# E and the slots' softmax transposed by the DMA crossbar as planes of 16-bit halves, with the softmax left undivided

## The chip, the cores and the metric

The kernel runs on one core of a Trainium2 chip. The metric is the device time of one execution in microseconds. All arithmetic is 32-bit floating point.

## The reference

The reference is one layer of gated slot attention followed by a feed-forward layer with a Hadamard transform in its middle, each with a residual and a layer norm behind it. The input x is 2 x 2048 x 512, with 16 heads of 64 key and 128 value channels and 64 slots a head.

```python
z = cumlogsumexp(s, axis=time);  g = exp(z[t-1] - z[t]);  p = exp(s - z)
hk[t] = hk[t-1] * g[t] + k[t] p[t]^T          # 64 keys x 64 slots
ok[t] = q[t] hk[t]
pv[t] = softmax(ok[t])                        # over the 64 slots
hv[t] = hv[t-1] * g[t] + p[t] v[t]^T          # 64 slots x 128 values
ov[t] = pv[t] hv[t]
o = ov * rsqrt(mean(ov**2) + 1e-5) * g_norm_weight * silu(gate)
x = layernorm(x + o @ Wo)
x = layernorm(x + fwht(silu(x W1^T) * (x W3^T)) @ W2^T)
```

## The kernel before

The attention part works on heads in four groups of four (`NG`, `HG`), and inside a group on 16 chunks of 128 positions (`NCB`), both batch entries of a chunk at once. That makes 64 steps. A step's four heads and two batch entries lie in tiles of 128 partitions x 4 x 128 words: `e` holds the exponentials of the slot logits (called E here), `r` the softmax over the slots, both with positions on the partitions. The products with the weights are Strassen-like: seven products a pair of matrices, named `q(1)` to `q(7)`, `v(1)` to `v(7)` and `o(1)` to `o(7)`. Their sums pass through three PSUM tags, c1 with two buffers, c2 and c3 with one; ACT copies the products 1, 5 and 6 out as `kept` (L458) and the product 4 (L460), and DVE adds the others (L463). c1 is used by q(1), q(6), q(7) and q(4) in turn, so q(7) waits for the `kept` copy of q(6).

`run(new, now, before, old)` (L998) writes out by hand the order of one pass of the loop: `now` is the current chunk, `before` the one before it, whose slots' softmax is ready, `old` the one two before, whose output is being finished. PE, DVE, ACT and POOL take their instructions in exactly this order; the order of SP, which issues all transfers, is set by the framework's own scheduling, and SP too is in order. After the four groups the feed-forward part runs, from about 2400 us on.

What the change touches, in the order of a pass:

- q products of `now` (L503). Between q(6) and q(7) stands `r_transposed` of `before` (L647): four PE transposes into a PSUM bank and an ACT copy to `rT`.
- `exp_s` (L508): DVE clamps, ACT exponentiates into `e2` and `e`, POOL adds the carried row `zc` to `e2` (L516).
- v(1), the transposed k, then small 64 x 64 matmuls: `scores` (L580), `scores2` of `before` (L655, reads `eT` and `rT`), `share_of_keys` (L590), `share_of_values` (L667).
- `e_transposed` (L553): four PE transposes into the same bank pair `ps[1]` that the masked scores were read from (L661), and an ACT copy to `eT`. It is used by the next pass.
- `running_sum` (L559), whose last row goes back to `zc` by two small transfers (L568); `slots` (L608), `values` (L678), `state_slots` (L617), `state_values` (L687, reads `rT`).
- `gated` (L696): squares of the values on ACT (L704), products with the gate on DVE (L706), the mean square plus epsilon to the power -1/2 on POOL (L710, L711), the scaling on POOL (L713).
- v(6), v(5), v(2), v(7); `softmax` (L622) on DVE with the exponential on ACT (L634); v(3); `softmax_sum` (L636) on DVE and POOL: the sum (L638), its reciprocal (L639), and the product of r with 1/z on POOL (L640).
- `o_transposed` of `before` (L724): eight PE transposes (L730), copied by ACT to `ob` (L427, L428), with sums on DVE (L432, L433) and POOL (L434, L435). Then `softmax_end` (L642), the product of r with the reciprocal (L644).
- v(4), `tanh` (L537) on ACT, then o(1), o(5) of `before` (L746, with the additions L742 on DVE), `silu` (L541) on DVE, o(2). o(1) reads `ob`. o(3), o(6), o(7), o(4) follow in the next pass. q(2) takes the c3 buffer that o(2) leaves.

Transfers on SP in a pass are the load of x for a later chunk (L473), loads and stores of the output rows (L721, L762), the two of `zc`, and those of the preparation of the feed-forward weights.

Of the kernel before, what the change touches and what calls it, by code (L numbers as in the profile page):

```python
# [8 lines left out]

F32 = mybir.dt.float32  # L10
AF = mybir.ActivationFunctionType
ALU = mybir.AluOpType
AX = mybir.AxisListType
PSUM = bass.MemoryType.PSUM

P = 128
# [4 lines left out]
DV = 128  # L21
M = 64
HG = 4
NG = H // HG
NQ = 4
TH = P // 2
HALVES = (slice(0, TH), slice(TH, P))
# [6 lines left out]
EPS = 1e-5  # L34
# [4 lines left out]
def gated_slot_attention_ffn_kernel(  # L39
# [13 lines left out]
    nc = tc.nc  # L53
# [7 lines left out]
    small = ctx.enter_context(tc.tile_pool(name="small", bufs=4))  # L61
    ident = const.tile([P, P], F32, name="ident")
    make_identity(nc, ident)


    causal3 = const.tile([P, P + TH], F32, name="causal")
    causal = causal3[:, 0:P]
    make_upper_triangular(nc, causal, val=1.0, diag=True)
    nc.gpsimd.tensor_copy(causal3[:, P:], causal3[:, 0:TH])
    mhalf = const.tile([P, 2 * NQ], F32, name="mhalf")  # L70
    nc.gpsimd.memset(mhalf, -0.5)
    gn = const.tile([P, 1], F32, name="gn")
    nc.sync.dma_start(out=gn, in_=gnw.rearrange("(p o) -> p o", o=1))

    half_gn = const.tile([P, 1], F32, name="half_gn")
    nc.gpsimd.tensor_scalar(half_gn, gn, 0.5, 0.0, ALU.mult, ALU.add)

    within = const.tile([P, TH], F32, name="within")
    for h in HALVES:
# [68 lines left out]
    xb, acc, res, h, wt = {}, {}, {}, {}, []  # L148
# [33 lines left out]
    def silu(h, at, src):  # L182
# [9 lines left out]
        gate, lin = v[:, :, :, 0:TQ], v[:, :, :, TQ:]  # L192
        nc.scalar.activation(o, gate, AF.Silu)

# [157 lines left out]
    with ExitStack() as att:  # L352
        keep = att.enter_context(tc.tile_pool(name="keep", bufs=1))
        c2 = att.enter_context(tc.tile_pool(name="c2", bufs=2))
        c1 = att.enter_context(tc.tile_pool(name="c1", bufs=1))
# [5 lines left out]
        ps = [pps.tile([P, 2, 512], F32, name=f"ps{i}") for i in range(2)]  # L361

        def bank(at, width=P):
            return ps[at // 2][:, at % 2].rearrange("p (i t) -> p i t", t=width)
# [8 lines left out]
        within_scores = [ps[1].rearrange("p j (k i t) -> p k j i t", k=2, t=TH)[:, k] for k in range(2)]  # L373
        pn = ps[1].rearrange("p j (k i m) -> p k j i m", k=2, m=M)[:, 1]

        pe = ps[1].rearrange("p j (k i t) -> p k j i t", k=2, t=P)[:, 0]

        hk = [keep.tile([P, NQ, M], F32, name=f"hk{s}") for s in range(3)]  # L380
# [6 lines left out]

        QUARTERS = [(i, j, HALVES[j], s, HALVES[s], HALVES[s ^ j]) for i in range(NQ) for j in range(2) for s in range(2)]
        OPENS = (1, 2, 5)

        def settle(sums):

            nc.scalar.copy(small.tile([P, 1], F32, name="seen", bufs=1), sums)
# [25 lines left out]
        def load_vg(g):  # L419
            return Weights("wvg", wvg[g])  # L420
# [44 lines left out]
        class Step:  # L465
# [42 lines left out]
            def exp_s(self):  # L508
# [3 lines left out]
                if not self.first:  # L512

                    self.e2 = c1.tile([P, NQ, P], F32, name="e2", tag="e2")
                    nc.scalar.activation(self.e2, self.e, AF.Exp)  # L515
                    nc.gpsimd.tensor_tensor(self.e2[0:1], self.e2[0:1], zc, ALU.add)  # L516
                nc.scalar.activation(self.e, self.e, AF.Exp)

# [31 lines left out]
                self.kr = c1.tile([P, NQ, P], F32, name="kr")  # L550
                nc.scalar.copy(self.kr, bank(0))

            def e_transposed(self):  # L553
                for i in range(NQ):
                    nc.tensor.transpose(pe[:, i // 2, i % 2], self.e[:, i, :], ident)
                self.eT = c2.tile([P, NQ, P], F32, name="eT")
                nc.scalar.copy(self.eT.rearrange("p (j i) t -> p j i t", j=2), pe)

            def running_sum(self):  # L559
                p = pch.tile([P, 512], F32, name="running", tag="c1", bufs=2).rearrange("p (i t) -> p i t", t=P)  # L560
# [73 lines left out]
                nc.scalar.activation(r, r, AF.Exp, scale=DK**-0.5)  # L634

            def softmax_sum(self):  # L636
                self.sm = small.tile([P, 2 * NQ], F32, name="sm")
                nc.vector.tensor_reduce(self.sm, self.r8, AX.X, ALU.add)  # L638
                nc.vector.reciprocal(self.sm, self.sm)  # L639
                nc.gpsimd.tensor_tensor(self.r, self.r, self.iz, ALU.mult)  # L640

            def softmax_end(self):  # L642
                smb = self.sm.rearrange("p (h o) -> p h o", o=1).to_broadcast([P, 2 * NQ, M])
                nc.vector.tensor_tensor(self.r8, self.r8, smb, ALU.mult)  # L644


            def r_transposed(self):  # L647
                for i in range(NQ):
                    nc.tensor.transpose(bank(0)[:, i, :], self.r[:, i, :], ident)
                self.rT = c1.tile([P, NQ, P], F32, name="rT")  # L650
                nc.scalar.copy(self.rT, bank(0))

            def scores2(self):
                for i, j, h, s, t, o in QUARTERS:
# [41 lines left out]
            def gated(self):  # L696

                sq = c1.tile([P, 2, NQ, DV], F32, name="sq", tag="big")
                self.gj = self.t2[:, :, HD:].rearrange("p q (j d) -> p j q d", d=DV)

                every = slice(0, P)
                moves = [(0, every, every), (1, HALVES[0], HALVES[1]), (1, HALVES[1], HALVES[0])]
                for j, to, at in moves:
                    nc.scalar.activation(sq[to, j], self.po[j][at], AF.Square)  # L704
                for j, to, at in moves:
                    nc.vector.tensor_tensor(self.gj[to, j], self.po[j][at], self.gj[to, j], ALU.mult)  # L706
                ss = small.tile([P, 2 * NQ], F32, name="ss")
                nc.vector.tensor_reduce(ss, sq.rearrange("p j q d -> p (j q) d"), AX.X, ALU.add)  # L708
                self.state()
                nc.gpsimd.tensor_scalar(ss, ss, 1.0 / DV, EPS, ALU.mult, ALU.add)  # L710
                nc.gpsimd.tensor_tensor(ss, ss, mhalf, ALU.pow)  # L711
                ssb = ss.rearrange("p (j q o) -> p j q o", j=2, o=1).to_broadcast([P, 2, NQ, DV])
                nc.gpsimd.tensor_tensor(self.gj, self.gj, ssb, ALU.mult)  # L713
# [284 lines left out]
        def run(new, now, before, old):  # L998


            def do(step, name, *args):
                if step is not None:
                    getattr(step, name)(*args)

            def main(name, k):

                if now is not None:
                    getattr(now, name)(k)
                elif before is not None:
                    for _ in range(FILL[name, k]):  # L1010
                        next(ups)

            def work_on(place):

                if not changes:
                    y["place"] = place
                    next(pieces[0], None)
# [30 lines left out]
            if changes:  # L1048
                nw["vg"].sums(0, nc.vector)
            main("q", 5)  # L1050
            work_on(3)
            if changes:
                nw["vg"].sums(1, nc.gpsimd)
            main("q", 6)
            do(old, "o", 6)
            do(before, "r_transposed")
            if changes:
                nw["vg"].sums(2, nc.vector)
            main("q", 7)
# [8 lines left out]
            if now is steps[-1]:  # L1068
                wt.append(load_w(0, 0))
                open_x("wqks", OUTER[:3], 3 * P)  # L1070
            do(now, "exp_s")
            do(old, "row_stats", 1)
            for f in late:
                f(0)
# [15 lines left out]
            do(before, "within2")  # L1090
            do(now, "share_of_keys")
            do(before, "share_of_values")
            do(now, "e_transposed")
            do(now, "running_sum")
            do(old, "row_stats", 0)
            do(old, "normalize")
# [35 lines left out]
                nw["o"].sums(2)  # L1132
                nw["o"].sums(3, nc.gpsimd)
            do(before, "o_transposed")
            do(now, "softmax_end")
            main("v", 4)
            if last:
                nw["vg"] = load_vg(g + 1)
            do(now, "tanh")
            if before is not None and before.first:  # L1140
                w["o"] = nw.pop("o")
# [46 lines left out]
    with tc.manual_schedule(  # L1188
# [11 lines left out]
        for u in range(NU):  # L1200
            if u:
                h = {}
# [89 lines left out]
```

## Time and profile before

| | us |
|---|---|
| median of 3 runs | 3513.03 (3512.81 to 3518.43) |
| span of the profiled execution | 3516.1 |
| attention part, about 0 to 2400: PE busy | 2364.9 |
| DVE, ACT, POOL busy in it | 1632.6, 807.1, 618.6 |
| feed-forward part, 2400 to 3516: PE busy | 1091.8 |

Groups of instructions that the change touches (line, engine, what, count, busy us, mean ns):

| line | engine | what | count | busy us | mean ns |
|---|---|---|---|---|---|
| L555 | PE | transposes of e | 256 | 42.0 | 287 |
| L649 | PE | transposes of r | 256 | 38.4 | 273 |
| L557 | ACT | copy to `eT`, 128x512 | 64 | 37.5 | 587 |
| L651 | ACT | copy to `rT`, 128x512 | 64 | 37.5 | 587 |
| L644 | DVE | r times the reciprocal, 128x512 | 64 | 77.9 | 1217 |
| L639 | DVE | reciprocal, 128x8 | 64 | 13.0 | 203 |
| L638 | DVE | sum, 128x512 to 128x8 | 64 | 43.9 | 686 |
| L539 | ACT | tanh, 128x1024 | 64 | 67.7 | 1058 |
| L393 | ACT | copy of 128x1 | 128 | 20.5 | 160 |

How to read it: matmuls are pipelined, so the mean of one is its latency and not the time that it takes from the stream; four transposes start 0.11 us apart. Busy shares are means over parts that have different limits. Idle time of an engine that nothing waits for costs nothing. A timeline row has the start, the time, the engine (PEld is the loading of weights on PE, SPq the issue of a transfer), the line, the operation, output and inputs, the count merged into the row, and in square brackets the idle time before it and what ended it.

### The profile page before, as it was taken

What the parts mean: (1) busy time and instruction counts of PE and PEld (TensorE: products, weight loads), DVE (VectorE), ACT (ScalarE), POOL (GpSimd) and SP (SyncE); (2) the same over time, 40 slices, a digit from 0 to 9 for tenths busy, and PEclk for the clock granted to TensorE, in tenths of its full rate; (3) what the DMA queues carried; (4) which work ended last, traced back from release to release, by engine and by line L of the source; (5) the groups of instructions that cost most, each with busy time, mean ns of one, the idle gap of its engine ahead of it and who ended that gap; (6) DMA issues with size and microseconds to landing.
All of it is one profiled execution on the core that took longest, in us unless ns stands there. A gap on an engine that the chain in (4) does not pass through costs nothing. (4 is left out here: it accounts for less than half of the span.)

```text
span 3516.1 us, 75258 instructions
## 1 busy us (share of the span) xinstructions
PE 3456.7 (98%) x31840; PEld 2702.8 (77%) x31840; DVE 2354.9 (67%) x3940; ACT 957.0 (27%) x1712; POOL 1144.2 (33%) x1069
## 2 busy tenths in 40 slices
PE   8999999999999999999999999998999999999998
PEld 6777777677777677677777777776888888888887
DVE  5777776665666765656766677777666756756756
ACT  3333333333333333333333333332111111111110
POOL 1222223221221331221332222223634643643544
PEclk9999999999999999999999999999999999999999
DMA  5334334221122232122222243347555544445431
GB/s 184 118 113 138 118 119 152 93 72 62 55 66 70 94 96 65 52 66 70 74 99 68 69 140 129 102 160 270 171 179 205 174 161 176 156 151 184 163 135 68
DMA packets 208833, 425.03 MB, mean 121 GB/s; under 512 B 19696, under 2 KB 120432, under 8 KB 207472
## 3 DMA queue, kind: packets, MB, share of 16 engines
q1 hardware_dynamic: 208496, 420.22, 35.7%
q8 instruction: 250, 4.10, 0.5%
q14 instruction: 87, 0.71, 0.1%
HBM read 297.47 MB, written 125.30 MB: 120 GB/s over the span
## 5 line engine op out<-in xcount | busy, mean ns | idle before, releaser
L529 PE MATMUL c<-wvg,xb 128*128 128x512 f32 x1792 | 812.7, 598 | 4.0 <-DVE wvg L412 2.0
L529 PEld LDWEIGHTS c<-wvg,xb 128*128 128x128 f32 x1792 | 322.1, 190 | 369.6 <-issue 291.9
L503 PE MATMUL c<-xb,wqks 128*128 128x128 f32 x3584 | 553.2, 277 | 15.7 <-DMA wqks<-wqks_blocks 9.6
L503 PEld LDWEIGHTS c<-xb,wqks 128*128 128x128 f32 x3584 | 479.9, 193 | 43.7 <-DVE rows L742 21.5
L218 DVE TENSOR_TENSOR accux<-c,accux 128x512 f32<-128x512 f32 x496 | 341.4, 691 | 180.9 <-PE c L237 163.5
L276 PE MATMUL dc<-w2t,hid 128*128 128x256 f32 x1792 | 455.3, 379 | 2.1 <-DVE res L283 2.1
L237 PE MATMUL c<-wvg,xb 128*128 128x256 f32 x1792 | 432.0, 380 | 6.1 <-DVE accux L218 5.3
L742 DVE TENSOR_TENSOR rows<-c,rows 128x256 f32<-128x256 f32 x448 | 181.7, 418 | 335.9 <-PE c L746 331.4
L237 PEld LDWEIGHTS c<-wvg,xb 128*128 128x128 f32 x1792 | 338.8, 190 | 56.9 <-DVE accux L218 9.1
L276 PEld LDWEIGHTS dc<-w2t,hid 128*128 128x128 f32 x1792 | 340.2, 190 | 49.5 <-DVE res L283 3.3
L503 PE MATMUL c<-wqks,xb 128*128 128x128 f32 x1792 | 347.4, 276 | 0.0
L463 DVE TENSOR_TENSOR t<-c,kept 128x384 f32<-128x384 f32 (+1 forms) x384 | 230.6, 611 | 155.6 <-PE c L503 147.5
L237 PE MATMUL c<-wqks,xb 128*128 128x256 f32 x1344 | 325.1, 380 | 5.2 <-DVE accux L218 2.3
L458 ACT COPY kept<-c 128x384 f32<-128x384 f32 (+1 forms) x384 | 203.5, 530 | 457.8 <-PE c L503 369.5
L516 POOL TENSOR_TENSOR e<-e,zc 1x512 f32<-1x512 f32 x60 | 76.4, 1273 | 710.0 <-ACT e L515 710.0
L237 PEld LDWEIGHTS c<-wqks,xb 128*128 128x128 f32 x1344 | 253.9, 190 | 44.0 <-DVE accux L218 5.0
L503 PEld LDWEIGHTS c<-wqks,xb 128*128 128x128 f32 x1792 | 273.0, 193 | 0.0
L283 DVE TENSOR_TENSOR res<-dc,res 128x256 f32<-128x256 f32 x448 | 189.2, 423 | 117.9 <-PE dc L276 107.3
L573 DVE RECIPROCAL iz<-z 128x256 f32<-128x256 f32 x128 | 223.9, 1749 | 44.6 <-ACT z L564 44.6
L710 POOL TENSOR_SCALAR ss<-ss 128x8 f32<-128x8 f32 x64 | 12.7, 198 | 685.3 <-DVE ss L708 685.3
L706 DVE TENSOR_TENSOR t<-po,t 64x512 f32<-64x512 f32 (+1 forms) x192 | 131.6, 685 | 95.6 <-ACT sq L704 94.3
L252 POOL TENSOR_TENSOR accw<-accw,accux 128x512 f32<-128x512 f32 x64 | 80.8, 1276 | 275.7 <-DVE accux L218 274.3
(189 smaller groups left out, 4975.7 us busy)
## 6 DMA issues: line engine op xcount, KB each, us to landing
xb<-w13s SPq DMA_DIRECT2D x112, 896.0 KB
xb<-xd SPq DMA_DIRECT2D x48, 896.0 KB
yd<-rows SPq DMA_DIRECT2D x128, 256.0 KB
w2t<-w2s SPq DMA_DIRECT2D x32, 896.0 KB
rows<-yd SPq DMA_DIRECT2D x100, 256.0 KB
xd<-xb SPq DMA_DIRECT2D x16, 896.0 KB
wvg<-fxd SPq DMA_DIRECT2D x16, 896.0 KB
w13s<-inner SPq DMA_DIRECT2D x96, 128.0 KB
```

The source lines that it names most:

```text
L218: nc.vector.tensor_tensor(into[:, b], s, (into if first is None else first)[:, b], ALU.add)
L237: nc.tensor.matmul(s[:, j * TQ : (j + 1) * TQ], lhsT=w[:, LEFT[k], j, :], rhs=right[:, RIGHT[k], :], start=(k in (1, 2, 5) and j == 0), st ...
L252: (nc.gpsimd if u or m == 6 else nc.vector).tensor_tensor(o, o, t["u"][:, b], ALU.add)
L276: nc.tensor.matmul(s, lhsT=h["hid"][:, i, LEFT[m], k * P : (k + 1) * P], rhs=h["w2"][:, i, RIGHT[m], :], start=(m in (1, 2, 5) and i == 0) ...
L283: nc.vector.tensor_tensor(r, s, r, ALU.add)
L458: nc.scalar.copy(self.kept[k], s)
L463: nc.vector.tensor_tensor(t[:, to], s, self.kept[other], ALU.add)
L503: nc.tensor.matmul(out[:, i * P : (i + 1) * P], lhsT=a, rhs=b, start=(k in OPENS and c == 0 and i == 0), stop=(c == 1), skip_group_check=True,
L529: nc.tensor.matmul(out, lhsT=self.xb[:, RIGHT[k], c, :], rhs=w["vg"].t[:, LEFT[k], c, :], start=(k in OPENS and c == 0), stop=(c == 1), sk ...
L573: nc.vector.reciprocal(self.iz[:, h], self.z[:, h])
L706: nc.vector.tensor_tensor(self.gj[to, j], self.po[j][at], self.gj[to, j], ALU.mult)
L742: nc.vector.tensor_tensor(y_, self.uo.sum(k), y_, ALU.add)
```

## The change

E and r are no longer transposed on PE. Each 32-bit word is split into its two 16-bit halves, the lower halves of a whole tile in one plane and the upper ones in another (`parts`: on POOL for E, on ACT for r). One DMA transpose a tile, issued from SP, sends both planes through the crossbar, which moves 16-bit elements, and an ACT copy joins the halves again (`e_joined`, `r_joined`). E's split is issued behind `exp_s` and joined in the next pass between q(5) and q(6). r's split is issued after v(4) and joined in the next pass where the PE transposes were.

r is no longer divided by its sum. The values come out larger by the factor of that sum, and so does the root of their mean square: epsilon times the square of the sum is added to the mean square in place of epsilon. That is `floor`: three small squares on ACT in `softmax_sum` (three since the two heads of a pair lie at different halves of the partitions), and one addition on POOL in `gated`. The reciprocal and the product on DVE go. The scratch that the program reserves for software-made DMA descriptors is set to 2048 bytes a partition.

```diff
+U16 = mybir.dt.uint16
...
-        pe = ps[1].rearrange("p j (k i t) -> p k j i t", k=2, t=P)[:, 0]
...
+        MOVES = [(0, slice(0, P), slice(0, P)), (1, HALVES[0], HALVES[1]), (1, HALVES[1], HALVES[0])]
+
+        def words(t):
+            return t.rearrange("p i t -> p (i t)").bitcast(U16).rearrange("p (c h) -> p h c", h=2)
...
-            def e_transposed(self):
-                for i in range(NQ):
-                    nc.tensor.transpose(pe[:, i // 2, i % 2], self.e[:, i, :], ident)
-                self.eT = c2.tile([P, NQ, P], F32, name="eT")
-                nc.scalar.copy(self.eT.rearrange("p (j i) t -> p j i t", j=2), pe)
+            def e_split(self):
+                parts = c1.tile([P, 2, NQ * P], U16, name="parts")
+                nc.gpsimd.tensor_copy(parts, words(self.e))
+                self.et = c1.tile([P, 2 * NQ, P], U16, name="et")
+                nc.sync.dma_start_transpose(out=self.et, in_=parts.rearrange("p h c -> p (h c)"))
+
+            def e_joined(self):
+                self.eT = c1.tile([P, NQ, P], F32, name="eT")
+                nc.scalar.copy(words(self.eT), self.et.rearrange("p (h i) t -> p h (i t)", h=2))
...
             def softmax_sum(self):
-                self.sm = small.tile([P, 2 * NQ], F32, name="sm")
-                nc.vector.tensor_reduce(self.sm, self.r8, AX.X, ALU.add)
-                nc.vector.reciprocal(self.sm, self.sm)
+                sm = small.tile([P, NQ, 2], F32, name="sm")
+                nc.vector.tensor_reduce(sm.rearrange("p q j -> p (q j)"), self.r8, AX.X, ALU.add)
                 nc.gpsimd.tensor_tensor(self.r, self.r, self.iz, ALU.mult)
-            def softmax_end(self):
-                smb = self.sm.rearrange("p (h o) -> p h o", o=1).to_broadcast([P, 2 * NQ, M])
-                nc.vector.tensor_tensor(self.r8, self.r8, smb, ALU.mult)
-            def r_transposed(self):
-                for i in range(NQ):
-                    nc.tensor.transpose(bank(0)[:, i, :], self.r[:, i, :], ident)
+                self.floor = small.tile([P, 2, NQ], F32, name="floor")
+                for j, to, at in MOVES:
+                    nc.scalar.activation(self.floor[to, j], sm[at, :, j], AF.Square, scale=EPS**0.5)
+            def r_split(self):
+                parts = c1.tile([P, 2, NQ * P], U16, name="parts_r")
+                nc.scalar.copy(parts, words(self.r))
+                self.rt = c1.tile([P, 2 * NQ, P], U16, name="rt")
+                nc.sync.dma_start_transpose(out=self.rt, in_=parts.rearrange("p h c -> p (h c)"))
+
+            def r_joined(self):
                 self.rT = c1.tile([P, NQ, P], F32, name="rT")
-                nc.scalar.copy(self.rT, bank(0))
+                nc.scalar.copy(words(self.rT), self.rt.rearrange("p (h i) t -> p h (i t)", h=2))
...
-                nc.gpsimd.tensor_scalar(ss, ss, 1.0 / DV, EPS, ALU.mult, ALU.add)
+                nc.gpsimd.tensor_scalar(ss, ss, 1.0 / DV, 0.0, ALU.mult, ALU.add)
+                nc.gpsimd.tensor_tensor(ss, ss, self.floor.rearrange("p j q -> p (j q)"), ALU.add)
                 nc.gpsimd.tensor_tensor(ss, ss, mhalf, ALU.pow)
...
             main("q", 5)
+            do(before, "e_joined")
...
             do(old, "o", 6)
-            do(before, "r_transposed")
+            do(before, "r_joined")
...
             do(now, "exp_s")
+            do(now, "e_split")
...
             do(before, "share_of_values")
-            do(now, "e_transposed")
             do(now, "running_sum")
...
             do(before, "o_transposed")
-            do(now, "softmax_end")
             main("v", 4)
...
+            do(now, "r_split")
             do(now, "tanh")
...
-    nc = bacc.Bacc("TRN2", target_bir_lowering=False, num_devices=1)
+    nc = bacc.Bacc("TRN2", target_bir_lowering=False, num_devices=1, dynamic_dma_scratch_size=2048)
```

More of the change, by code (lines that the diff above doesn't have):

```diff
@@ L699, in gated @@
                 self.gj = self.t2[:, :, HD:].rearrange("p q (j d) -> p j q d", d=DV)
-                every = slice(0, P)
-                moves = [(0, every, every), (1, HALVES[0], HALVES[1]), (1, HALVES[1], HALVES[0])]
-                for j, to, at in moves:
+                for j, to, at in MOVES:
                     nc.scalar.activation(sq[to, j], self.po[j][at], AF.Square)
-                for j, to, at in moves:
+                for j, to, at in MOVES:
                     nc.vector.tensor_tensor(self.gj[to, j], self.po[j][at], self.gj[to, j], ALU.mult)
```

## The prediction

> **What bounds the kernel now.** I read the page's parts 1 and 2 first, then PE's waits, then one step of the chunk loop in the timeline, and last the group rows for prices.
>
> ```profile
> PE 3456.7 (98%) x31840; PEld 2702.8 (77%) x31840; DVE 2354.9 (67%) x3940; ACT 957.0 (27%) x1712; POOL 1144.2 (33%) x1069
> PEclk9999999999999999999999999999999999999999
> PE c L746 <- ACT ob L427: 5.0, 8, 1.3
> PE c L503 <- DVE rows L742: 5.2, 9, 1.2
> SPq L721 <- DMA yd<-rows: 173.0, 73, 6.0
> ```
>
> PE is busy for 98% of the span at a full granted clock, and the longest waits in its list are a few us each over the whole run. So work taken from PE is worth its full price, and any new wait of PE costs its full length. The loop takes about 37.6 us a step (L730 comes at 1529.07 and again at 1566.68). A step, where the change touches it:
>
> ```profile
> 1504.32 0.48 ACT L458 COPY kept<-c 128x384 f32<-128x384 f32 x1 [0.86 <-PE c L503]
> 1504.98 0.60 PE L649 MATMUL ps<-ident,r 128*128 128x128 f32 x4
> 1505.42 0.61 PE L503 MATMUL c<-xb,wqks 128*128 128x128 f32 x4
> 1513.42 0.56 PEld L580 LDWEIGHTS ps<-t 64*64 64x64 f32 x32 [0.33 <-issue]
> 1515.99 0.42 PEld L555 LDWEIGHTS ps<-ident,e 128*128 128x128 f32 x4 [0.31 <-DVE a L661]
> 1516.48 1.03 PE L562 MATMUL running<-e,causal 128*128 128x256 f32 x4
> 1517.44 0.56 PEld L608 LDWEIGHTS ps<-e,a 64*64 64x64 f32 x32 [0.33 <-ACT eT L557]
> ...
> 1529.07 1.08 PE L730 MATMUL ps<-ident,t 128*128 128x128 f32 x8
> 1529.99 1.88 PE L529 MATMUL c<-wvg,xb 128*128 128x512 f32 x4
> 1530.55 0.63 ACT L634 ACTIVATE r<-r 128x512 f32<-128x512 f32 x1 [5.84 <-DVE r L633]
> 1531.09 0.57 ACT L427 COPY ob<-ps 128x512 f32<-128x512 f32 x1
> 1531.21 0.69 DVE L638 TENSOR_REDUCE sm<-r 128x8 f32<-128x512 f32 x1 [0.16 <-ACT r L634]
> 1531.71 2.85 PE L746 MATMUL c<-wo__11903,ob 128*128 128x256 f32 x12
> 1531.90 0.33 SPq L473 DMA_DIRECT2D xb<-xd  x1
> 1532.04 1.29 POOL L640 TENSOR_TENSOR r<-r,iz 128x512 f32<-128x512 f32 x1 [3.04 <-DVE sm L638]
> ```
>
> The reader should see two things. The transposes L649 and L555 sit in an unbroken PE stream. And just before L746, ACT runs the exponential (L634) and at once the copy of `ob` (L427), which PE consumes 0.05 us after it ends, while DVE is still summing the exponentials: that sum ends at 1531.90, 0.19 us after PE has begun L746. At the other steps the sum ends 0.19 us after L746 begins in the first three groups of heads and 0.14 us after in the fourth.
>
> **What is removed from PE.** Four r transposes: 1504.98 to 1505.42, 0.44 us. Four E transposes: 1515.99 to 1516.48, 0.49 us. Ahead of them PE waits for L661 to free the bank: the last L667 matmul starts 0.34 us before L555, where the same change of tile size elsewhere (L687 to L529) takes 0.20, so 0.14 us goes too. The 0.33 before L608 stays, since L580 has the same 0.33 with no releaser. Removed: 1.07 us a step. On ACT the copies L651 and L557 (587 ns each) go, on DVE the reciprocal L639 (203) and the product L644 (1217): both come after the sum. DVE's relief is worth little: at some 40 steps PE waits 0.14 us in the q stage for L742, which stands behind silu on DVE. With DVE freed I count that 0.14 as gone, 0.09 us a step on average.
>
> **What is added, and what hides it.** (1) The split of E on POOL, 1024 elements: below, a 128x64 copy took 0.23 us; above, L713 took 1.90 for 1024 elements with two inputs. POOL is idle from 1513.33 (end of L516) to 1525.10, so neither end reaches the path. (2) On POOL one 128x8 addition ahead of the power, about 0.2 us by L710's 198 ns, with 0.08 of gap. L713 now ends only 0.07 us before L730, so L730 would slip 0.28; a longer wait comes 2.6 us later and contains it, so I count nothing; without that wait it would cost 0.28 x 62 = 17 us. (3) The r split on ACT, as long as L539's 128x1024 (1.06 us), is put after v's copy L460 and before tanh. Its POOL input (L640) is done before ACT gets there. It pushes tanh to 3.1 us and silu's end to 4.3 us after L746's start; L742 of o(2) ends at 4.75, q(2) needs it at 4.9. Hidden by 0.15 us; what is queued behind it on ACT is q(1)'s `kept` copy, due at 4.1. (4) Joining E on ACT stands between the `kept` copies of q(5) and q(6). The former ends 1503.46; plus 1.06 gives 1504.52, so the q(6) copy ends 1505.02 rather than 1504.80, and q(7) starts 1505.08 instead of 1504.98, its new natural place after the r transposes go: 0.10 us of stall. Bounds: at L458's 0.58 for 512 words, none; at twice L539, 1.2. I take 0.10. (5) Joining r on ACT replaces L651 and is 0.47 longer; nothing of PE's waits for it there, unless its transfer is late (below).
>
> (6) The three squares `floor` on ACT. In the built order they stand after L634 and before L427. They need DVE's sum, so ACT, and the `ob` copies queued behind, now wait for it, and L746 behind these. From L746's present start: sum 0.19, releaser to ACT 0.03 (L634 to L638), three squares, two gaps of 0.02 as between the L704 squares, 0.02, the copy 0.57, and 0.05 to PE. A square of four elements: L517 (512) took 632 ns and L539 (1024) 1058, a line that reaches 0.21 at four elements; below, L393's one-element copy took 0.16; above, L428 (256) took 0.38. With 0.21 the first L746 starts 0.19 + 0.03 + 0.63 + 0.04 + 0.02 + 0.57 + 0.05 = 1.53 us late. DVE's chain to the sum starts at PE's L687 and moves along with it, so earlier PE work doesn't widen this.
>
> The Trainium skill (ScalarE: Activation LUTs, What ACT_TABLE_LOAD costs) says that an immediate-scale ACTIVATE has 186 ns fixed and that back-to-back ones overlap by 93 ns. By that the three squares are an estimated 0.38 us and the stall 1.24; the L704 squares here follow each other with a gap of 0.02 and no overlap.
>
> (7) Two crossbar transposes of 256 KB on SP. E's is issued about 1515 and stands before the later yd store, row load and the two zc transfers (issued 1518.20, needed by L516 some 30 us later); its result is joined 25 us later. r's stands behind L473's xb load and ahead of the row load; it is issued 2.1 us after L746's start. Its join must begin by 14.0 us after it, since then L460 (ending 1510.12, and v(1) starting 1510.31 needs its bank) would be late: 11.9 us of room. The trace has no such transfer. Below: SP's waits for a plain 256 KB yd store (the last line of the first block) are 173.0 us in 73, 2.4 us each. Above: the trace's packets of 4 bytes took 9 ns, and 131,072 of them over 16 engines would be 74 us. The built instruction moves blocks of 16 rows, so pieces of 32 bytes: 8,192 over 16 engines at 9 to 19 ns (4 and 256 byte packets) are 4.6 to 9.6 us. I take 6 us: hidden.
>
> The Trainium skill (VectorE: DVE Perf Modes, The three transpose paths and Rules for kernel authors) speaks against the change: 390 ns on TensorE against 1309 ns through the crossbar for 128x128 of 16 bits, with TensorE preferred where PSUM will do. Eight in a row are an estimated 10.5 us, still inside the room.
>
> **Sum.** -1.07 - 0.09 + 1.53 + 0.10 = +0.47 us a step, x 62 steps that have both a current and a preceding chunk: +29 us. The profiled execution spans 3516.1, so 3545; the runs' median 3513.03 is 3.1 lower, so 3542. The FFN part (from about 2400 us) is untouched. Ends: squares at 0.16 and no q(7) stall, +0.22 a step, 3527; squares at 0.38, +0.98, 3574.
>
> **Rivals.** *The gate is cheap* (faster): the squares overlap or the sum comes earlier. Even squares of no length leave the wait for the sum: 0.19 + 0.03 + 0.02 + 0.57 + 0.05 = 0.86. With no q(7) stall the step is then 1.16 - 0.86 = 0.30 better, 19 us, 3494. It decides from three squares under 0.3 us together. For it: only the extrapolation prices them. Against: the 0.16 of L393 three times is 0.48. *The crossbar is late* (slower): r lands more than 11.9 us after issue, ACT stands in the join, and the copy L460 and v(1) behind it. Each us over is 62 us; at 20 us, 8 x 62 = 500, 4040. For it: the 74 us bound; against: the 16-row blocks. *The change moves nothing*: gate and removed transposes cancel, squares at 0.16 and L730's or q's slack taken up elsewhere, 3513. For it: the terms are equal in kind and each known to about 0.15 us a step, 9 us.
>
> **How the numbers follow.** The gate as costed 0.66, cheap gate 0.12, crossbar late 0.11, cancelling 0.11. A measurement of this kernel can tell about 0.2%, 7 us, from no change. Faster: 0.12, the cheap gate. Same: 0.11 plus 0.03 from the low end of the gate, 0.14. Slower: 0.74. The range reaches from 3510, within the cancelling case, to 3580, above the gate's high end; the likeliest case alone has 3527 to 3574. Outside are the cheap gate and the late crossbar.
>
> **What would show it.** In PE's waits a new row of L746's line behind the `ob` copy, near 62 times and 1.2 to 1.6 us each, some 95 us in all; ACT's idle before `floor` ended by the sum on DVE. The 512 PE transposes of L555 and L649 gone. q(7) behind ACT's `kept` by about 0.1 us. If PE's new waits are instead behind the join of r, the crossbar is late; if L746 waits under 0.9 us, the gate was cheap and the forecast is wrong.

## The result, and the profile after

The changed kernel takes 3563.5 us (median of 4 runs, 3560.8 to 3564.2) against 3514.5 for the kernel before, measured beside it: a ratio of 1.013 (95% interval 1.0116 to 1.0145). The profiled execution spans 3561.4 us, 45.3 more than before.

The page's first part and, from PE's and ACT's lists of waits (total us, times, longest), the rows that are new:

```profile
PE 3430.7 (96%) x31328; PEld 2659.9 (75%) x31328; DVE 2289.2 (64%) x3812; ACT 1126.2 (32%) x1968; POOL 1196.5 (34%) x1197
```
```profile
PE c L758 <- ACT ob L431: 77.0, 63, 4.0
...
PE c L533 <- DVE t L717: 7.5, 12, 0.7
```
```profile
ACT floor L652 <- DVE sm L647: 49.9, 64, 2.0
```

PE has 512 instructions fewer and 26 us less to do, and yet the span is longer: PE stands still. L758 is o(1) (L746 before), L431 the copy to `ob` (L427 before), L647 the sum. The second row, v (L533) behind the gate's products (L717), is all in the fourth group and comes up again in experiment 4. The step that the prediction showed, after the change (timeline):

```profile
1549.05 1.09 PE L742 MATMUL ps<-ident,t 128*128 128x128 f32 x8
...
1549.98 1.88 PE L533 MATMUL c<-wvg,xb 128*128 128x512 f32 x4
...
1550.20 0.63 ACT L643 ACTIVATE r<-r 128x512 f32<-128x512 f32 x1 [5.78 <-DVE r L642]
...
1550.86 0.69 DVE L647 TENSOR_REDUCE sm<-r 128x8 f32<-128x512 f32 x1
1551.58 0.64 ACT L652 ACTIVATE floor<-sm 128x4 f32<-128x4 f32 x3 [0.75 <-DVE sm L647]
...
1552.24 0.58 ACT L431 COPY ob<-ps 128x512 f32<-128x512 f32 x1
...
1552.88 2.86 PE L758 MATMUL c<-wo__12005,ob 128*128 128x256 f32 x12 [1.02 <-ACT ob L431]
```

Read down ACT: the exponential ends at 1550.83, ACT waits 0.75 us for DVE's sum, does three squares, and only then the copy that o(1) needs. Before, the copy began 0.09 us before the exponential's end.

To see where the rest of the 45 us lies, I took the starts of PE's stages out of the timeline of all 62 steps, here the median step of each group of heads and the sum over all steps, after less before:

| stretch on PE | before, groups 1, 2, 3, 4 | after | sum over 62 steps, us |
|---|---|---|---|
| o transposes to o(1) | 2.63, 2.64, 2.64, 2.59 | 3.84, 3.84, 3.84, 4.00 | +78.8 |
| o(1) to the k transposes (the q stage; r was transposed here) | 17.06, 17.68, 17.91, 17.65 | 16.60, 17.45, 17.45, 17.47 | -28.1 |
| scores2 to `slots` (E was transposed here) | 3.51 in all | 2.98 in all | -31.6 |
| `slots` to v(6) | 2.94 in all | 2.94 to 3.15 | +1.6 |
| v(6) to the next o transposes | 8.69, 8.69, 8.69, 9.01 | 8.94, 8.94, 8.94, 9.61 | +19.9 |
| before the first and after the last step | | | +5.4 |

In groups 2 and 3 the q stage has two lengths, since about half of the steps there also prepare feed-forward weights on PE; their medians are of the longer kind. The stretch from the k transposes to scores2 is 1.91 in both kernels.

These make 46.1 (PE's first to last start). A step in the first group grew from 36.75 to 37.22 us, the +0.47 of the forecast; in the fourth group it grew by 1.30.

The prices of the new work (groups of instructions, each shape apart: busy us, mean ns, idle time before them) and SP's issue of the crossbar transfers (ns min/median/max):

```profile
L664 ACT COPY rT<-rt 128x1024 uint16<-128x1024 uint16 x64 | 86.9, 1358 | 0.1
L566 ACT COPY eT<-et 128x1024 uint16<-128x1024 uint16 x64 | 86.5, 1352 | 0.0
...
L658 ACT COPY parts_r<-r 128x1024 uint16<-128x1024 uint16 x64 | 68.3, 1068 | 0.2 <-POOL r L648 0.2
...
L652 ACT ACTIVATE floor<-sm 64x4 f32<-64x4 f32 x128 | 26.1, 204 | 1.5
...
L652 ACT ACTIVATE floor<-sm 128x4 f32<-128x4 f32 x64 | 13.2, 206 | 49.9 <-DVE sm L647 49.9
```
```profile
L562 SPq DMA_TRANSPOSE et<-parts x64: 1232/1242/2719, 24.6 to 2421.5; - x64
```

The joins have no idle time before them that a transfer ended: ACT never waited for the crossbar. By the trace's packets (1024 of 256 bytes a transfer) r's transfers had landed 2.6 us after their issue in the median and 7.7 at worst, E's 3.4 and 5.9.

### The profile page after: what moved, and what is told of

The parts are those of the page before. It is cut to its first block, busy times and chain, and to the rows that moved or that the text cites. A ratio compares the mean times of both kernels' runs of the same rounds, so it can differ in the third digit from the quotient of the medians.

```text
span 3561.4 us, 74715 instructions
## 1 busy us (share of the span) xinstructions
PE 3430.7 (96%) x31328; PEld 2659.9 (75%) x31328; DVE 2289.2 (64%) x3812; ACT 1126.2 (32%) x1968; POOL 1196.5 (34%) x1197
## 5 line engine op out<-in xcount | busy, mean ns | idle before, releaser
L533 PE MATMUL c<-wvg,xb 128*128 128x512 f32 x1792 | 812.9, 598 | 10.9 <-DVE t L717 7.5
L533 PEld LDWEIGHTS c<-wvg,xb 128*128 128x128 f32 x1792 | 322.3, 190 | 376.3 <-issue 292.3
L507 PE MATMUL c<-xb,wqks 128*128 128x128 f32 x3584 | 554.8, 277 | 12.3 <-DMA wqks<-wqks_blocks 8.9
L507 PEld LDWEIGHTS c<-xb,wqks 128*128 128x128 f32 x3584 | 482.5, 192 | 48.2 <-ACT kept L462 23.1
L754 DVE TENSOR_TENSOR rows<-c,rows 128x256 f32<-128x256 f32 x448 | 189.7, 423 | 420.1 <-PE c L758 413.8
L507 PE MATMUL c<-wqks,xb 128*128 128x128 f32 x1792 | 347.2, 275 | 0.0
L507 PEld LDWEIGHTS c<-wqks,xb 128*128 128x128 f32 x1792 | 273.0, 193 | 0.0
L717 DVE TENSOR_TENSOR t<-po,t 64x512 f32<-64x512 f32 (+1 forms) x192 | 131.6, 685 | 95.6 <-ACT sq L715 94.4
```

What stands on the lines that cost most here:

```text
L507: nc.tensor.matmul(out[:, i * P : (i + 1) * P], lhsT=a, rhs=b, start=(k in OPENS and c == 0 and i == 0), stop=(c == 1), skip_group_check=True,
L533: nc.tensor.matmul(out, lhsT=self.xb[:, RIGHT[k], c, :], rhs=w["vg"].t[:, LEFT[k], c, :], start=(k in OPENS and c == 0), stop=(c == 1), sk ...
L754: nc.vector.tensor_tensor(y_, self.uo.sum(k), y_, ALU.add)
```

## The experiments

Times are medians; "before" is the kernel before, run beside each. Experiments 1, 2, 4 and 5 were run together, as were 6 to 9, and 10 and 11.

**1. The gate away.** The squares are moved behind tanh:

```diff
+            def floors(self):
+                sm = self.sm
                 self.floor = small.tile([P, 2, NQ], F32, name="floor")
...
             do(now, "tanh")
+            do(now, "floors")
```

> The changed kernel with the three squares (floor) moved behind tanh on ACT, out of the way of the copies to ob. Theory (the gate in front of o(1) is the loss): the stretch from the o transposes to o(1) falls from 3.84 us back to 2.64 in the first three groups, and PE's waits for ACT's ob copy from 77.0 us to under 10. But ACT then reaches r's split earlier, which stands ahead of tanh and reads POOL's product; that ends some 1.6 us after o(1) starts, so tanh, silu and o(2)'s additions come later and up to 0.65 us a step can go to a wait of q(2). The 0.25 us that POOL's addition costs stays. So 3563 - 1.2 x 62 = 3489 with no new wait and 3529 with all of it. Rival (the crossbar transfers and the joins are the loss, and the gate merely shows up where something else would): 3555 to 3570, with the wait turning up at another line.

Measured: 3488.6 against 3519.0 before, ratio 0.992 (0.9904 to 0.9934), 75 us less than the changed kernel. PE's wait for the copy (L762 is o(1) here):

```profile
PE c L762 <- ACT ob L431: 4.3, 5, 1.2
```

The stretch to o(1) is back at 2.65 us. Of the feared wait of q(2) little came: r's split waits 0.52 us for POOL in the median, and the weight loads of q wait 19.8 us in 42 for o(2)'s additions, a row that the changed kernel doesn't have. That makes the q stage 6.3 us longer over all steps than in the changed kernel, and still 0.3 us a step shorter than before. One thing, the place of three squares, turns the change from a loss into a gain. The 0.26 that the o transposes come late stayed.

**2. The gate alone.** The undivided softmax and its floor, with E and r transposed on PE as before (the diff less `e_split`, `e_joined`, `r_split` and `r_joined`).

> The kernel before with only the undivided softmax and its floor; E and r are still transposed on PE. Theory: nothing is taken from PE, and each step pays the gate (1.20 us in front of o(1), 1.41 in the fourth group) and POOL's addition (0.25 in front of the o transposes): 1.45 to 1.5 x 62 = 90 to 93 us more, 3604 to 3608. Rival (the crossbar part is the loss): not over 3520. Prediction's own sums: 1.53 x 62 = 95 less 0.09 x 62 for the DVE product that goes, 3603.

Measured: 3608.4 against 3519.0, ratio 1.0258 (1.0243 to 1.0273), 89 us more.

```profile
PE c L750 <- ACT ob L433: 81.1, 63, 4.0
```

The loss is there in full without a single crossbar transfer. The stretch to o(1) is 3.89 us in groups 1 to 3 and 4.07 in the fourth, the o transposes come 0.26 late in groups 1 to 3 and not at all in the fourth. The setting of the scratch, which is in every changed kernel, was not tried by itself; it is in this one too, where the gate explains the loss.

**3. What the gate consists of.** The squares stay where the change put them and read the row maxima:

```diff
-                    nc.scalar.activation(self.floor[to, j], sm[at, :, j], AF.Square, scale=EPS**0.5)
+                    nc.scalar.activation(self.floor[to, j], mx[at, :, j], AF.Square, scale=EPS**0.5)
```

> The changed kernel with the three squares where the change put them, but reading the row maxima, which DVE finished before the exponential, in place of the sums: the floor's value is another, the work is the same, and only ACT's wait for the sum is gone. It splits the gate in two. Theory (the gate is a wait of 0.75 us for the sum and 0.64 us of squares, of which PE's own work up to o(1) covers 0.19): the squares then begin 0.02 after the exponential ends, the copy follows, and o(1) starts 1.78 + 0.02 + 0.64 + 0.02 + 0.58 + 0.06 = 3.10 us after the o transposes where it was 3.84: 0.74 x 62 = 46 us less, 3518. Rival (the squares are the price, the wait lies beside other work): 3550 or more. Rival 2 (the wait is all of it): 3490.

Measured: 3501.6 against 3517.0, ratio 0.996 (0.994 to 0.997): 62 us less than the changed kernel, where 46 were expected and 73 by the rival that gives the wait all of it. The stretch to o(1) is 2.97 us, so the wait for the sum was 0.87 of the 1.20, and the squares the remaining 0.33. In the timeline the step has

```profile
1513.61 0.63 ACT L643 ACTIVATE r<-r 128x512 f32<-128x512 f32 x1 [5.78 <-DVE r L642]
1514.14 0.62 ACT L653 ACTIVATE floor<-mx 128x4 f32<-128x4 f32 x3
1514.79 0.59 ACT L431 COPY ob<-ps 128x512 f32<-128x512 f32 x1
```

and shows what was missed: the first square begins 0.10 us before the exponential ends. So the wait for the sum cost this overlap besides its own length: 0.75 and 0.10 of the 0.87. The sum over the steps falls by 54 us (0.87 x 62); 6 of the other 8 lie in the drain after the last step, the rest is not traced to one place.

**4. E alone.** The kernel before with E through the crossbar, the softmax divided and r transposed on PE (`e_split` and `e_joined` of the diff alone).

> The kernel before with only E sent through the crossbar; the softmax is divided and r is transposed on PE. Theory (in the fourth group DVE bounds the stretch from scores2 to v(2), elsewhere PE does): 0.53 us a step in the 47 steps of the first three groups and nothing in the fourth, less 0.1 a step if q(7) waits for the join: 3514 - 20 to 25 = 3489 to 3494. Rival 1 (PE bounds everywhere): 0.53 x 62 = 33 us, 3481. Rival 2 (the transfers disturb other work): 3514 or more.

Measured: 3486.9 against 3519.0, ratio 0.992 (0.990 to 0.993), 32 us less. In the medians that is what the rival gives that lets PE bound everywhere; but its baseline was 5 us above the one that the expectation started from, and the interval of 6 us to either side doesn't tell the two apart. The steps do. The stretch of E falls by 0.53 us in every step; in groups 1 to 3 the step falls by as much (36.75 to 36.21 in the first), and in the fourth it stays at 37.60. There v(6) to the o transposes grew by the same 0.53. Over all steps the two sum to -32.9 and +6.1. DVE in such a step (timeline), with the first and last row of the same chain in the kernel before behind it:

```profile
2120.62 0.69 DVE L594 TENSOR_TENSOR a<-ps,within 128x512 f32<-128x512 f32 x1 [0.70 <-PE ps L665]
2121.23 0.68 DVE L671 TENSOR_TENSOR a<-ps,within 128x512 f32<-128x512 f32 x1
2121.83 0.94 DVE L612 TENSOR_TENSOR hk<-hk,pk 128x256 f32<-128x256 f32 x2
2122.68 0.68 DVE L612 TENSOR_TENSOR hv<-hv,ps 128x512 f32<-128x512 f32 x1
2123.28 0.69 DVE L87 BATCH_NORM_STATS2 st<-rows 128x6 f32<-128x512 f32 x1
2124.01 0.18 DVE L89 BATCH_NORM_AGGREGATE mv<-st 128x2 f32<-128x6 f32 x1
2125.14 1.00 DVE L96 TENSOR_SCALAR rows<-rows,mv,lrs 128x512 f32<-128x512 f32 x2 [0.95 <-POOL lrs L92]
2126.05 1.75 DVE L583 RECIPROCAL iz<-z 128x256 f32<-128x256 f32 x1
2127.72 2.05 DVE L716 TENSOR_TENSOR t<-po,t 128x512 f32<-128x512 f32 x3
```
```profile
2128.40 7.13 PE L534 MATMUL c<-wvg,xb 128*128 128x512 f32 x16 [0.59 <-DVE t L716]
```
```profile
2150.68 0.69 DVE L584 TENSOR_TENSOR a<-ps,within 128x512 f32<-128x512 f32 x1 [0.70 <-PE ps L655]
...
2157.77 2.05 DVE L706 TENSOR_TENSOR t<-po,t 128x512 f32<-128x512 f32 x3
```

From the masked scores (L594) to the gate's products (L716) DVE has no gap but the wait for POOL inside the normalization of the output rows, which is only there in the fourth group. PE then waits for the first of these products. In the kernel before the same chain from the same start takes 7.09 us (L584 to L706), here 7.10: what is taken from PE behind the chain's start can't move its end.

**5. Both through the crossbar, softmax divided.** The kernel before with both transposes through the crossbar; there is no floor, and the division stays. r's split is put behind tanh:

```diff
             do(now, "tanh")
+            do(now, "r_split")
```

> The kernel before with both E and r sent through the crossbar; the softmax is divided as before, so there is no floor, and r's split stands behind tanh on ACT since DVE's product ends some 2.9 us after o(1) starts. Theory: 0.53 x 47 + 0.45 x 62 = 53 us less, 3461; if q(7) waits for the joins 0.1 a step, 3467. If the split holds up the kept copy of q(1), due 4.1 us after o(1) starts, up to 0.3 a step more, 3486. Rival (the transfers are the loss): 3540 or more.

Measured: 3473.7 against 3519.0, ratio 0.988 (0.986 to 0.989), 45 us less: the gain is smaller than either of the first two forecasts. E gives 0.53 a step again, the q stage only 0.28 where r's four transposes had taken 0.44 (experiment 9 finds the rest).

**6. The crossbar twice.** The changed kernel with each transfer issued again into a tile that nothing reads:

```diff
                 nc.sync.dma_start_transpose(out=self.et, in_=parts.rearrange("p h c -> p (h c)"))
+                nc.sync.dma_start_transpose(out=twice, in_=parts.rearrange("p h c -> p (h c)"))
```

> The changed kernel with each of the 128 crossbar transfers issued twice, the second into a tile that nothing reads. Theory (the transfers are hidden: they land 2.6 and 3.4 us after issue, 12 to 25 us ahead of their joins): same time within 0.2%, 3556 to 3570, with no wait of ACT for a transfer. Rival (the transfers or SP's issue of 1.25 us each take part in the loss, by contention or by delaying the other transfers): each us that they cost would cost again, 3590 or more.

Measured: 3565.3, against 3563.5 with one of each. The second issues on SP (min/median/max ns, then first and last start) took 1.87 us for E in the median where the first take 1.23:

```profile
L564 SPq DMA_TRANSPOSE twice<-parts x64: 1261/1868/3807, 25.8 to 2425.8; - x64
```

and no stretch of the step changed by more than 0.01 us in the medians of the groups, `slots` to v(6) aside, which scatters. A second set of transfers costs nothing here that the runs can tell.

**7. One operation less on POOL.** On top of experiment 1, the mean's division by 128 goes into ACT's squares:

```diff
-                    nc.scalar.activation(sq[to, j], self.po[j][at], AF.Square)
+                    nc.scalar.activation(sq[to, j], self.po[j][at], AF.Square, scale=DV**-0.5)
...
-                nc.gpsimd.tensor_scalar(ss, ss, 1.0 / DV, 0.0, ALU.mult, ALU.add)
                 nc.gpsimd.tensor_tensor(ss, ss, self.floor.rearrange("p j q -> p (j q)"), ALU.add)
```

> The kernel with the squares behind tanh, and one operation less on POOL: the squares of the values are scaled by 1/128 on ACT, so that POOL only adds the floor and takes the power, as many operations as before the change. Theory (POOL's added operation stands on the chain to the o transposes in the first three groups, where they come 0.26 us later; in the fourth group DVE bounds this stretch): 0.26 x 47 = 12 us less than the 3488.6 measured with the squares behind tanh, 3476; the o transposes then come 8.69 us after v begins in the first three groups and still 9.4 to 9.6 in the fourth. Rival (the 0.26 has another cause, such as POOL's split of E): 3489, stretch still 8.95.

Measured: 3485.9 against 3488.6 in experiment 1, where 3476 was expected; beside the kernel before the ratios are 0.991 and 0.992, so no gain is clear of noise. The 0.26 went as expected (v(6) to the o transposes 8.69 in groups 1 to 3), but in the first and third group the q stage grew by 0.29. The row of PE's waits that grew from 3.4 us in 7 waits:

```profile
PE c L507 <- DVE rows L757: 11.2, 41, 0.7
```

q(2) now waits for o(2)'s additions, which stand on DVE behind silu, which waits for tanh, which stood behind r's split on ACT. As long as POOL's addition held up the o transposes, this chain had more time: one stall had covered part of another. In experiment 11, with tanh ahead of the split, the row is down to 0.9 us in 3 waits.

**8. The normalization later.** Experiment 5 with the normalization of the output rows (fourth group) moved on DVE behind the gate's products:

```diff
-            do(old, "normalize")
-            do(old, "store_rows")
...
             do(before, "gated")
+            do(old, "normalize")
+            do(old, "store_rows")
```

> The kernel with both through the crossbar and the softmax divided (3473.7), with the normalization of the output rows, which is there in the fourth group alone, moved on DVE from behind the running sum to behind the products with the gate. Theory (in the fourth group DVE bounds the stretch from the second scores to v(2): its wait of 0.95 for POOL and the two normalizations of 1.0 stand ahead of the gate's products): v(2) no longer waits, and the step of that group falls by about 0.53 us, from 37.32 to 36.8, x 13 steps = 7 us: 3467. Rival (what E saves is lost in the fourth group to something else, such as the transfers): step stays 37.3, 3474. Were DVE's sum of the exponentials to become late instead, the o transposes to o(1) would grow over 2.6 us.

Measured: 3484.3, 11 us more than experiment 5 (ratios to before 0.9905 and 0.9877); 7.6 us of the difference lie in the steps and 5.7 after the last one. v no longer waits (9.54 to 8.69 in the fourth group), and o(1) comes 0.89 later after the o transposes (2.59 to 3.48):

```profile
PE c L761 <- ACT ob L432: 12.5, 17, 1.2
```

The softmax's exponential now stands behind the normalization through DVE's order, and the `ob` copies behind the exponential, so the same row as in the changed kernel is back. Both sides were thus partly right: DVE does bound the way to v(2), and the saving does not stay, since DVE bounds the way to o(1) as well. Moving work along an engine that bounds the whole stretch gained nothing.

**9. E's join behind r's.** On top of experiment 5:

```diff
             main("q", 5)
-            do(before, "e_joined")
...
             do(before, "r_joined")
+            do(before, "e_joined")
```

> The kernel with both through the crossbar and the softmax divided (3473.7), with the join of E moved on ACT from between the kept copies of q(5) and q(6) to behind the join of r. Theory (the join of 1.36 us delays the kept copy of q(6), which q(7) waits for, since r's transposes no longer stand between them): the stretch from o(1) to the k transposes falls by 0.11 us a step, from 17.37 to 17.26 in the fourth group, x 62 = 7 us: 3467. Rival (the missing part of r's saving lies elsewhere): 3474, stretch unchanged. The joins then end at most 3 us after the kept copy and are needed some 8 us after it, so no new wait.

Measured: 3462.0 against 3473.7 in experiment 5; the q stage is 0.22 us shorter, twice what was expected. Experiment 5, PE from o(6) into q(7), then the same in experiment 9:

```profile
2099.00 1.03 PE L761 MATMUL c<-wo__17417,ob 128*128 128x256 f32 x4
2099.98 0.71 PE L508 MATMUL c<-xb,wqks 128*128 128x128 f32 x4
2100.53 0.39 PE L508 MATMUL c<-wqks,xb 128*128 128x128 f32 x2
```
```profile
2090.76 1.03 PE L761 MATMUL c<-wo__17417,ob 128*128 128x256 f32 x4
2091.62 0.61 PE L508 MATMUL c<-xb,wqks 128*128 128x128 f32 x4
2092.07 0.39 PE L508 MATMUL c<-wqks,xb 128*128 128x128 f32 x2
```

q(7) starts 0.98 after o(6) with the join in between and 0.86 without; and its first four matmuls then take 0.55 up to the next group in place of 0.45. Here a wait of 0.12 costs 0.22. It stands in the list of the weight loads, again experiment 5 and then 9; the changed kernel has the same row (23.1 us in 64):

```profile
PEld c L508 <- ACT kept L463: 23.1, 64, 0.8
```
```profile
PEld c L508 <- ACT kept L463: 1.5, 2, 0.8
```

**10. The normalization on POOL.** On top of experiment 9, in the fourth group:

```diff
-                        normalize(self.rows[b], self.stats[b])
+                        nc.gpsimd.tensor_scalar(self.rows[b], self.rows[b], *self.stats[b], ALU.subtract, ALU.mult)
```

> The kernel with both through the crossbar, the softmax divided and E's join behind r's (3462.0), with the two normalizations of the output rows (fourth group alone) on POOL instead of DVE. POOL is idle for 6.0 us there; at the 1.28 us of its 128x512 product the two take some 2.6. Theory (DVE bounds the whole way from the second scores to the exponential of the softmax in the fourth group, so that only taking work from it gains there): both its wait for POOL of 0.95 and the two normalizations of 1.0 go; v to the o transposes falls from 9.54 to the 8.69 of the other groups without the o transposes to o(1) growing, step from 37.11 to 36.26, 0.85 x 13 = 11 us: 3451. Rival (as when the normalization was moved on DVE, 0.89 of it comes back in front of o(1)): 3460 or more.

Measured: 3457.4 against 3462.0 in experiment 9; ratio to before 0.983 (0.982 to 0.984). That lies between the 3451 expected and the 3460 at which the rival began, and the medians alone don't decide. The stretches do: the step of the fourth group falls from 37.11 to 36.34 us (36.26 expected), v(6) to the o transposes to 8.69, and o(1) loses only 0.06 of it. So DVE did bound this group. Of the 10 us that this stretch gives over the group, the span has 6 and the median 5: the part after the last step took 3.2 back, and whether that is scatter, the granted clock of the drain or a cost of POOL's slower work (2.08 us each, below) isn't settled.

**11. The same, undivided.** Squares behind tanh and r's split, one operation on POOL, E's join behind r's, the normalization on POOL:

```diff
             do(now, "tanh")
+            do(now, "r_split")
+            do(now, "floors")
```

> The same arrangement with the softmax left undivided: squares and r's split behind tanh, the floor as POOL's only addition, E's join behind r's, normalization on POOL. It tells what leaving out the division is worth once neither gate nor waits stand in its way. Theory: DVE's 1.4 us a step for reciprocal and product lie beside PE and are worth little, at most the 4.8 us in which PE waits for the additions of o behind silu in the divided form: 3446 to 3451, that is 0 to 5 below the divided form. Rival (the division bounds something): over 8 us below it. Rival 2 (the squares still cost): above it.

Measured: 3442.7 us (3438.8 to 3443.2) against 3517.0 before, ratio 0.979 (0.978 to 0.980). It is the fastest of all, 2.1% below the kernel before and 3.4% below the changed one, and 15 us below the divided form, where at most 5 was expected. The sum over the q stage fell by 14.0 us. The waits that went are not in PE's list but in that of its weight loads; the divided form (experiment 10) has

```profile
PEld c L508 <- DVE rows L757: 20.9, 43, 1.3
```

and the undivided form (there L507) 2.7 us in 4. The expectation had looked at the matmuls' row alone (4.7 us in 9). The gain is not the same everywhere: 0.23 us in most steps of the first and third groups, 0.5 to 0.9 in most steps around a change of group, and nothing in half of the second group and nearly all of the fourth, where this wait was not there.

## Why the prediction was right, and where it was not

It said slower, by 29 us, through a wait of o(1) behind the `ob` copy. It is slower by 45 to 49, through that wait.

**The gate** was right in mechanism and nearly in size. Its 1.53 us held the 0.28 by which L730 slips; measured, o(1) comes 1.20 after that and the slip is 0.25 (experiment 2 has both without a crossbar): 1.45 in groups 1 to 3. Summed over all steps that is 78.8 + 48 x 0.25 = 91 us against 95 (48 of the 62 steps; in the 14 of the fourth group another chain bounds the way to the o transposes). The squares took 0.204 us each against 0.21. Of the two prices weighed for them, the L704 row was right: three took 0.64, with no overlap among them, so the 93 ns of the Trainium skill (ScalarE: Activation LUTs, What ACT_TABLE_LOAD costs) is not seen there. It is seen, at 0.10, between the exponential and what follows it without a wait (experiment 3). That the slip is contained in the later wait held too: its price without this cover, given as 17 us, would have been smaller by what experiment 7 found hidden under it.

**E's transposes** were the step that failed. The prediction wrote that PE is busy 98% of the time, "so work taken from PE is worth its full price", and multiplied by 62. The 0.63 was 0.53: of the two changes of tile size it removed, the first running-sum matmuls pay 0.10 for one (1.06 us to `slots`, from 1536.04 to 1537.10, in place of 0.96). And in the fourth group, 14 of the steps, it was worth nothing, because DVE bounds the way from the scores to v(2) there (experiments 4 and 10). 39.1 us were counted; -31.6 + (19.9 - 12.0) = -23.7 came, 12.0 being the slip of 48 x 0.25. The view of before had shown it: this stretch took 9.01 us in the fourth group and 8.69 in the others, so PE was already being held there by 0.32.

**r's transposes, the join and DVE's relief** came out right in sum (-26.7 counted, -28.1 measured) by luck: two errors cancelled. The join before q(6)'s copy costs 0.22, not 0.10 (it takes 1.35 us, not 1.06, and the wait slows the matmuls behind it; experiment 9). DVE's relief is worth 0.23 a step, not 0.09 (14.0 us over 62 steps, experiment 11). The wait is in before's list of the weight loads:

```profile
PEld c L503 <- DVE rows L742: 21.5, 43, 1.6
```

The prediction counted 0.14 at some 40 such steps; taking the wait away gave 0.23 at most of them, and more around the changes of group. Both prices come from other arrangements (experiment 11 also moves the squares and frees r's split from DVE's product), and the changed kernel doesn't part them; but experiment 2, which has the relief and no join, shortens the q stage by 12.0 us over the steps.

That r's split is hidden by 0.15 us held only while the gate stood in front: with the gate gone, q(2) waited for what lies behind the split (experiment 1), and for longer with POOL's operation gone too (experiment 7).

**The crossbar** was hidden, with more room than assumed: landed 2.6 and 3.4 us after issue, 7.7 at worst, where 6 was taken and 11.9 to spare; issuing each twice changed nothing clear of noise. The 6 came from 8,192 pieces of 32 bytes, and the trace shows 1,024 packets of 256. The Trainium skill's figure for one block (VectorE: DVE Perf Modes, The three transpose paths), by which eight in a row would be an estimated 10.5 us, gives over three times what these transfers took. Its advice to transpose on TensorE where PSUM will do (the same page, Rules for kernel authors) doesn't hold here, where PE bounds and SP and the DMA engines don't: both through the crossbar alone gained 45 us (experiment 5).

**The rest of the difference.** Of the 16.3 us by which the span missed (3545 against 3561.4), E is 15.4, the gate -4, r's part -1, and the ends with `slots` to v(6) 7, less 0.8 by which PE's starts grew more than the span. The other 5 between 3542 and the measured median is which executions were compared: the profiled one of before was 3.9 above the median of its four, that of after at its own, and the median of three that the prediction started from was 1.5 below that of four. So of the 20 us between 29 and 49, E makes 15 and the choice of executions about 5; the rest nearly cancels.

## What to carry to other kernels

Read the bound of each stage, not of the whole: a stage that is longer in one part of the loop than in another, with PE doing the same in both, is held by something else, and what is taken from PE there is worth nothing. Before an instruction is put into an engine's order, ask what it waits for and what stands behind it: three 0.2 us squares cost 79 us in front of a copy that PE needs, of which nearly three quarters were the wait, and left no such wait when they stood behind it. Look for waits in the rows of the weight loads too, and when a stall is removed, ask which chain had been living off its time.

## What the runs showed of the hardware

A copy of 128x1024 16-bit elements on ACT takes 1.07 us when it reads with a stride of two and writes densely (L658), and 1.35 when it reads densely and writes with a stride (L566, L664). Normalizing 128x512 takes 0.54 us on DVE (L95 of the kernel before) and 2.08 on POOL (experiment 10):

```profile
L773 POOL TENSOR_SCALAR rows<-rows,mv,lrs x32: 2071/2076/2081, 1843.6 to 2382.7; 128x512 f32<-128x512 f32 x32
```

In the drain after the last steps the granted clock fell in the changed kernel, where it had been full before. The same 20 us of the span, in which the kernel before is some 40 us further on in its work, after and before (window, length, busy time of each engine, granted clock, DMA share, GB/s):

```profile
2440.00:2460.00 20.00, 15.94 (x61) 12.57 (x60) 13.68 (x24) 10.04 (x16) 6.24 (x7) 0.83 0.79 261
```
```profile
2440.00:2460.00 20.00, 18.12 (x90) 14.99 (x89) 12.41 (x21) 4.11 (x7) 5.08 (x9) 1.00 0.70 264
```

Experiment 2, without the crossbar, has such dips as well (0.83 from 2480 to 2500), and experiments 3 and 4, with crossbar transfers, have none before the very end, so the transfers neither are needed for them nor suffice; the cause stays open. The part after the last step is 4.6 us longer than before in the changed kernel and 6.4 in experiment 2, and 0.4 in experiment 4, so the dips are worth an estimated 6 us at most.
